# A hybrid attention and FP4 feed-forward kernel: the feed-forward input is turned by DMA, scales are spread by two DMAs, the quantizer works in place with its reciprocals in PSUM

## The chip, the cores and the metric

The kernel runs on one core of a Trainium2 chip. The metric is the device time of one execution in microseconds; less is better. Engines are named as in the profile: PE (TensorE, matmuls; PEld its weight loads), DVE (VectorE), ACT (ScalarE), POOL (GpSimd), SP (SyncE, which issues all DMAs here).

## The reference

x has 4 sequences of 2048 tokens of 256 values, all f32. Four residual steps are applied to it, each on the layer norm of x:

```python
x = x + attn_a(layernorm(x))   # v projection, scaled per head by s / s (s from random feature maps of q and k)
x = x + ffn(layernorm(x))
x = x + attn_b(layernorm(x))   # linear attention across the 4 sequences, per token and head
x = x + ffn(layernorm(x))

def fp4_quant_dequant(x):                     # blocks of 16 along the last dimension
    scale = max(max(abs(xb)) / 6.0, 1e-12)
    q = GRID[searchsorted(MID, abs(xb / scale))] * sign(xb) * scale

def ffn(x):                                   # 256 -> 704 -> 256
    h = silu(fq(x) @ fq(w_gate).T) * (fq(x) @ fq(w_up).T)
    return fq(h) @ fq(w_down).T
```

Here `fq` is `fp4_quant_dequant`. Both the input of the feed-forward part (256 wide) and its hidden values (704 wide) are quantized at run time.

## The kernel before

Tokens go through in 16 groups (`NJ`) of 128 tokens x 4 sequences (`S`). A first pass over x takes the statistics that the first attention needs and quantizes the weights (`quantize`). Then, for each group, come `attention_a`, `ffn_in` and four `ffn_tile`s, `attention_b`, and again `ffn_in` and four `ffn_tile`s: 32 inputs and 128 tiles in all.

Nothing is issued in the order in which the code stands. Each step is an operation of a planner (`Plan.op`): an engine, a cost, a due time (`BEGIN` of its group and stage, plus its place in the stage) and the tiles that it reads and writes. `Plan.order` runs through a model of the engines, takes at each moment the ready operation with the earliest due time, hands out buffers from pools (`plan.pool`, `tiles`), and so writes one fixed order for each engine. `port=True` marks operations that the planner keeps from running on DVE and POOL at the same time. The table `BEGIN` holds six due times for each of the 16 groups.

PSUM has eight banks: four in the pool `mm` (gate and up results, `hidden`), four in `bank` (everything else that PE writes).

The quantizer `to_grid` is a chain: DVE takes the maxima of blocks (L1215) and their reciprocals (L1225), multiplies the values by them (`over_scales`, L390, two SBUF inputs), ACT takes absolute values into bf16 steps (`to_steps`, L396), and DVE rounds by two passes (`to_sum` L403, `from_sum` L406). The values lie in blocks of 17 (`xn`, `h`; the 17th keeps the maxima above zero), the results go to tiles of their own (`qax`, `qa`).

What happens after it differs:

- *The input* (`ffn_in`): the grid values stay f32 in `qax`. ACT multiplies the maxima by 1/6 (L1270), POOL multiplies the values by the scales (`times_scales`, L1278), PE turns them with eight 128x128 transposes into two banks, and ACT copies these into `turned` (`turn`, L1152 and L1159).
- *A tile* (`ffn_tile`): the grid values go to bf16 (`qm`), and one DMA transpose turns them (`gT`, L1513). The maxima are turned by PE (L1294), scaled by ACT on their way to `sT` (L1302), and spread by six DMAs over 16 partitions each into `hqT` (`spread`, L1311). POOL multiplies the two (L1522), and PE takes the product through the down projection (L1559). The last four tiles go another way, with POOL and PE transposes (L1535).

Layer norms are `take_var` (ACT, L348) and `root` (a chain of eight small POOL operations, `take_rstd`).

## Time and profile before

| | |
|---|---|
| three runs | 1486.37, 1483.82, 1482.01 us; median 1483.82 |
| the profiled execution | 1483.54 us, of which 1481.7 us from its first to its last instruction (the span) |
| mean granted TensorE clock | 0.998 of full |
| PE busy | 1436.8 us, 97% |
| DVE, ACT, POOL busy | 1344.0 (91%), 794.4 (54%), 769.7 us (52%) |
| DMA | 33.8% of 16 engines' time; 744 spread DMAs and 124 transposes into tiles |

Busy times are unions of the instructions' intervals on an engine; a group's mean is the time from start to end of one instruction, and pipelined instructions overlap. L numbers are lines of the kernel before. "A <- B" in a list of waits says that A's engine sat idle until B ended.

### The profile page before, as it was taken

Reading aid. Unit: us, or ns where it says so; the run is one execution under the profiler, and the core shown is the slowest. Engines: PE = TensorE matmul, PEld = TensorE weight load, DVE = VectorE, ACT = ScalarE, POOL = GpSimd, SP = SyncE. Lnnn points to the kernel's source line nnn. Section 1 sums busy time; section 2 is a strip of 40 time slices with the busy share of each in tenths; the row PEclk is TensorE's granted clock in tenths of the full one; section 3 lists DMA queues with packets and bytes.
Section 4 is the critical chain, followed back from the end, with each engine's and each line's share of the span. In section 5 each row is a group of like instructions: output and inputs, shape, how many; then the busy total and the mean of one; then the engine's idle time right before and its main releaser. Section 6 shows DMA issues by size and latency. Waiting matters only on the chain.

```text
span 1481.7 us, 19959 instructions
## 1 busy us (share of the span) xinstructions
PE 1436.8 (97%) x5742; PEld 998.8 (67%) x5742; DVE 1344.0 (91%) x2139; ACT 794.4 (54%) x1693; POOL 769.7 (52%) x787
## 2 busy tenths in 40 slices
PE   7989999999999999999999999999999999999998
PEld 6745667666767667676666666676677667676776
DVE  6799999999899999988997999988999898999995
ACT  6656557742674545544376455557525744546332
POOL 5344556534763646454644537556365654564532
PEclk9999999999999999999999999999999999999999
DMA  8402422124324334143432433231344134322451
GB/s 258 120 0 37 65 44 38 35 51 81 61 45 83 65 63 79 36 86 55 89 74 34 65 58 68 46 67 27 60 96 78 38 62 74 63 56 40 92 90 40
DMA packets 220990, 96.87 MB, mean 65 GB/s; under 512 B 108240, under 2 KB 220624, under 8 KB 220880
## 3 DMA queue, kind: packets, MB, share of 16 engines
q1 hardware_dynamic: 220880, 95.60, 33.8%
q8 instruction: 45, 0.74, 0.2%
q14 instruction: 65, 0.53, 0.1%
HBM read 18.09 MB, written 8.39 MB: 18 GB/s over the span
## 4 chain that ended last, share of the span: by engine, by line
PE 67%; DVE 13%; POOL 7%; DMA 5%; issue 4%; ACT 3%; SPq 1%; POOLq 0%; ACTq 0%; DVEq 0%
PE bank L1455 30%; PE bank L1175 17%; PE bank L1559 17%; PE bank L1152 3%; DMA gT<-qm 3%; POOL hqT L1522 2%; DVE qa L403 1%; DVE qm L406 1%; DVE pp L1666 1%; DVE h L1487 1%; DVE sh L1215 1%; DVE qa L390 1%; DVE x L342 1%; POOL norms_f L358 1%; PE bank L1294 1%
## 5 line engine op out<-in xcount | busy, mean ns | idle before, releaser
L1455 PE MATMUL bank<-wguT,turned 128*128 128x352 f32 x2048 | 634.2, 459 | 2.0 <-ACT sil L1476 2.0
L1455 PEld LDWEIGHTS bank<-wguT,turned 128*128 128x128 f32 x2048 | 380.4, 190 | 201.5 <-issue 11.8
L1522 POOL TENSOR_TENSOR hqT<-hqT,gT 128x768 f32<-128x768 f32 x124 | 228.8, 1849 | 258.6 <-DMA gT<-qm 117.4
L1559 PE MATMUL bank<-wdT,hqT 128*128 128x256 f32 x1536 | 350.9, 380 | 7.1 <-POOL hqT L1522 6.6
L1559 PEld LDWEIGHTS bank<-wdT,hqT 128*128 128x128 f32 x1536 | 288.7, 190 | 66.8 <-POOL hqT L1522 16.7
L1476 ACT ACTIVATE sil<-bank 128x352 f32<-128x352 f32 x256 | 115.7, 457 | 131.5 <-PE bank L1455 123.3
L396 ACT ACTIVATE qm<-qa 128x704 bf16<-128x704 f32 (+2 forms) x136 | 106.0, 780 | 96.9 <-DVE qa L390 74.6
L1487 DVE TENSOR_TENSOR h<-sil,bank 128x352 f32<-128x352 f32 x256 | 128.4, 506 | 29.6 <-ACT sil L1476 15.5
L1774 POOL TENSOR_TENSOR pp<-vg,sc 128x1024 f32<-128x1024 f32 x64 | 138.6, 2179 | 22.2 <-DVE tok L1795 20.1
L403 DVE SCALAR_TENSOR_TENSOR qa<-qm,qa 128x704 f32<-128x704 bf16 (+2 forms) x136 | 141.0, 1039 | 7.7 <-ACT qm L396 7.4
L390 DVE SCALAR_TENSOR_TENSOR qa<-sh,h 128x704 f32<-128x704 f32 x128 | 133.4, 1047 | 0.5
L406 DVE SCALAR_TENSOR_TENSOR qm<-qm,qa 128x704 bf16<-128x704 bf16 x124 | 126.8, 1025 | 0.2
L1175 PE MATMUL bank<-wvz,turned 128*128 128x512 f32 x256 | 119.8, 608 | 6.9 <-ACT turned L1159 3.5
L1175 PE MATMUL bank<-wqkB,turned 128*128 128x512 f32 x256 | 120.4, 593 | 1.8 <-ACT turned L1159 1.8
L1159 ACT COPY turned<-bank 128x512 f32<-128x512 f32 x160 | 87.5, 584 | 64.2 <-PE bank L1152 63.8
L1215 DVE TENSOR_REDUCE sh<-h 128x44 f32<-128x748 f32 x128 | 118.3, 924 | 2.0
L1278 POOL TENSOR_TENSOR qax<-qax,sx 128x1024 f32<-128x1024 f32 x32 | 68.1, 2128 | 90.2 <-DVE qax L406 73.8
L348 ACT ACTIVATE dev<-x,norms_f 128x256 f32<-128x256 f32 x128 | 64.7, 506 | 50.5 <-DVE x L342 48.1
L1175 PEld LDWEIGHTS bank<-wvz,turned 128*128 128x128 f32 x256 | 47.6, 193 | 56.9 <-issue 42.5
L1666 DVE TENSOR_TENSOR pp<-qk 128x1024 f32<-128x1024 f32 x64 | 83.2, 1312 | 0.6 <-ACT qk L1654 0.6
L1302 ACT ACTIVATE sT<-bank 44x128 f32<-44x128 f32 x124 | 32.8, 267 | 92.7 <-PE bank L1294 50.8
L384 ACT ACTIVATE xn<-x,norms_f 128x256 f32<-128x256 f32 x128 | 67.5, 593 | 21.3 <-POOL norms_f L378 18.2
(193 smaller groups left out, 2079.3 us busy)
## 6 DMA issues: line engine op xcount, KB each, us to landing
hqT<-sT SPq DMA_DIRECT2D x620, 64.0 KB
x<-in_L_attn_a_x_dram SPq DMA_DIRECT2D x23, 512.0 KB
out_dram<-x SPq DMA_DIRECT2D x64, 128.0 KB
hqT<-sT SPq DMA_DIRECT2D x124, 32.0 KB
gT<-qm SPq DMA_TRANSPOSE x124
hqT<-in_L_ffn_w_down_dram SPq DMA_DIRECT2D x2, 352.0 KB
hqT<-in_L_ffn_w_gate_dram SPq DMA_DIRECT2D x5, 128.0 KB
hqT<-in_L_ffn_w_up_dram SPq DMA_DIRECT2D x5, 128.0 KB
```

What stands on the lines that cost most here:

```text
L390: nc.vector.scalar_tensor_tensor(blocks(a), over_blocks(rs), -6.0 * BELOW, src, ALU.mult, ALU.mult)
L396: nc.scalar.activation(m, a, AF.Abs, scale=UP)
L403: nc.vector.scalar_tensor_tensor(a, m, FLOOR, a, ALU.max, ALU.add)
L406: nc.vector.scalar_tensor_tensor(a if to is None else to, m, FLOOR, a, ALU.max, ALU.subtract)
L1175: nc.tensor.matmul(bank.ap[:, :n], lhs.ap[:, c, s * P : (s + 1) * P], w[:, c, :], start=(c == 0), stop=(c == KC - 1),)
L1215: lambda: nc.vector.tensor_reduce(q.ap[:, 0, :], src.ap, AX.X, ALU.max, apply_absolute_value=True),
L1455: nc.tensor.matmul(bank.ap[:, :HF], xqT.ap[:, c, s * P : (s + 1) * P], w[:, c, cols], start=(c == 0), stop=(c == KC - 1),)
L1476: lambda g=g, sil=sil: nc.scalar.activation(sil.ap, g.ap[:, :HF], AF.Silu),
L1487: lambda u=u, sil=sil, half=half: nc.vector.tensor_mul(h.ap[:, half * FB // 2 : (half + 1) * FB // 2, :BLK], blocks(sil.ap), blocks(u.ap[: ...
L1522: lambda: nc.gpsimd.tensor_mul(hqT.ap, hqT.ap, gT.ap),
L1559: nc.tensor.matmul(o.ap[:, :D], hqT.ap[:, i, :], wdT[:, i, :], start=(i == 0), stop=(i == 5),)
L1774: nc.gpsimd.tensor_mul(pv.ap.rearrange("p t (n e) -> p t n e", e=HD), vg.ap[:, :, :D].rearrange("p t (n e) -> p t n e", e=HD), over_blocks ...
```

## The change

The input of the feed-forward part now goes the way of the tiles: its grid values go to bf16 (`qmx`, in place of the steps), one DMA transpose of eight blocks turns them (`gTx`), the scales are turned by PE and spread by DMA into `turned`, and POOL multiplies there. The spread is made of two DMAs in place of six, for tiles and inputs: ACT first writes each scale twice (by 1/6), PE turns these, ACT copies the turned scales out of PSUM in pieces of 32 rows beside each other, and each DMA spreads 16 of the rows, eight times each, with all pieces in one run. The order of chunks in `hqT` follows from that.

The quantizer works in place, in its 17-wide blocks; `qa` and `qax` are gone, `h` has five buffers and `xn` two. The reciprocals of the maxima go to PSUM: the eighth bank is taken out of the pool `bank` (three are left) and holds two places for inputs (`rx`) and four for tiles (`rh`); `over_scales` is no longer marked `port=True`. The weights' quantizer works in place too, and one of the two banks of the first pass's sums comes from `mm`. `dev`, into which `take_var` writes values that nobody reads, is bf16. Some operations name a buffer as their "place", so that it is handed out earlier. The table `BEGIN` has new values throughout.

```diff
         for j in range(NJ)
     }
-    dev = one([P, D], "dev")
+    dev = one([P, D], "dev", dtype=BF16)
 
...
@@ -388,7 +388,7 @@
     def over_scales(a, src, rs):
 
         nc.vector.scalar_tensor_tensor(
-            blocks(a), over_blocks(rs), -6.0 * BELOW, src, ALU.mult, ALU.mult
+            a, over_blocks(rs), -6.0 * BELOW, src, ALU.mult, ALU.mult
         )
 
     def to_steps(m, a):
@@ -416,24 +416,27 @@
         return made
 
     plan.pool("mm", banks[:4])
-    plan.pool("bank", banks[4:])
+    plan.pool("bank", banks[4:7])
+    plan.pool("rx", [banks[7][:, 64 * i : 64 * i + 64] for i in range(2)])
+    plan.pool("rh", [banks[7][:, 128 + FB * i : 128 + FB * (i + 1)] for i in range(4)])
     plan.pool("x", xs_of)
     tiles("turned", 6, [P, KC, GT], fp)
 
-    floored = tiles("xn", 1, [P, S * D // BLK, BLK + 1], fp)
-    floored += tiles("h", 3, [P, FB, BLK + 1], fp)
-    tiles("qax", 2, [P, S * D], fp)
+    floored = tiles("xn", 2, [P, S * D // BLK, BLK + 1], fp)
+    floored += tiles("h", 5, [P, FB, BLK + 1], fp)
     tiles("qmx", 1, [P, S * D], fp, BF16)
-    tiles("sx", 2, [P, 3, S * D // BLK], fp)
+    tiles("sx", 2, [P, 4 * S * D // BLK], fp)
     tiles("sil", 2, [P, HF], fp)
-    tiles("qa", 3, [P, FF], fp)
 
     for t in tiles("qm", 2, [P, 6 * P], fp, BF16):
         nc.gpsimd.memset(t[:, FF:], 0.0)
     tiles("gT", 2, [P, 6, P], fp, BF16)
 
-    tiles("sT", 2, [FB, P], fp)
-    tiles("sh", 4, [P, 3, FB], fp)
+    tiles("sT", 2, [32, 3, P], fp)
+    tiles("sTx", 1, [32, S, P], fp)
+    tiles("gTx", 1, [P, S * KC, P], fp, BF16)
+    for t in tiles("sh", 4, [P, 2 * FB + 96], fp):
+        nc.gpsimd.memset(t[:, FB : FB + 96], 0.0)
     for t in tiles("hqT", 3, [P, 6, P], fp):
         nc.gpsimd.memset(t[P // 2 :, 5, :], 0.0)
     tiles("tok", 1, [P, S, D], fp)
...
@@ -748,17 +751,17 @@
                 "DVE",
                 0.15 + n / 1000.0,
                 at + 1,
-                lambda: over_scales(ap(a), blocks(ap(raw)), sc(2)),
-                [(raw, 0), (w, 0)],
-                [(a, 0)],
+                lambda: over_scales(blocks(ap(raw)), blocks(ap(raw)), sc(2)),
+                [(w, 0)],
+                [(raw, 0)],
...
@@ -1106,22 +1109,22 @@
 
 
     BEGIN = [
-        (-378, -314, -1376, -1348, 17, -996),
-        (-171, 99, -285, -130, -472, 322),
...
+        (-991, -209, -170, -1464, -194, -968),
+        (-54, 117, -88, -713, 84, 124),
...
@@ -1204,70 +1207,84 @@
                     port=True,
                 )
 
-        def to_grid(at, src, parts, a, m, q, us, to=None):
-
-            v = blocks_of(src)
-            n = us["n"]
+        def to_grid(at, b, parts, m, q, us, to):
+
+
+            n, nb = us["n"], us["n"] // BLK
+            r = plan.buf("rx" if n > FF else "rh")
+
+            def v():
+                return b.ap[:, :, :BLK]
+
+            def mv():
+                return blocks(m.ap[:, :n])
+
             op(
                 "DVE",
                 us["amax"],
                 at,
                 lambda: nc.vector.tensor_reduce(
-                    q.ap[:, 0, :], src.ap, AX.X, ALU.max, apply_absolute_value=True
+                    q.ap[:, :nb], b.ap, AX.X, ALU.max, apply_absolute_value=True
                 ),
-                [(src, i) for i in parts],
+                [(b, i) for i in parts],
                 [(q, 0)],
             )
             op(
                 "DVE",
                 us["recip"],
                 at + 0.5,
-                lambda: nc.vector.reciprocal(q.ap[:, 2, :], q.ap[:, 0, :]),
+                lambda: nc.vector.reciprocal(r.ap, q.ap[:, :nb]),
                 [(q, 0)],
-                [(q, 2)],
+                [(r, 0)],
             )
             op(
                 "DVE",
                 us["pass"],
                 at + 1,
-                lambda: over_scales(a.ap, v(), q.ap[:, 2, :]),
-                [(src, i) for i in parts] + [(q, 2)],
-                [(a, 0)],
-                port=True,
+                lambda: over_scales(v(), v(), r.ap),
+                [(r, 0)],
+                [(b, i) for i in parts],
             )
             op(
                 "ACT",
                 us["abs"],
                 at + 2,
-                lambda: to_steps(m.ap[:, :n], a.ap),
-                [(a, 0)],
+                lambda: to_steps(mv(), v()),
+                [(b, i) for i in parts],
                 [(m, 0)],
             )
             op(
                 "DVE",
                 us["pass"],
                 at + 4,
-                lambda: to_sum(a.ap, m.ap[:, :n]),
+                lambda: to_sum(v(), mv()),
                 [(m, 0)],
-                [(a, 0)],
+                [(b, i) for i in parts],
                 port=True,
             )
             op(
                 "DVE",
                 us["pass"],
                 at + 4.1,
-                lambda: from_sum(a.ap, m.ap[:, :n], to and to.ap[:, :n]),
-                [(a, 0), (m, 0)],
-                [(to or a, 0)],
+                lambda: from_sum(v(), mv(), blocks(to())),
+                [(b, i) for i in parts] + [(m, 0)],
+                [(us["into"], 0)],
                 port=True,
             )
 
...
-        def scales_turned(at, q, dst):
-
-
-            bank, sT = plan.buf("bank"), plan.buf("sT")
+        def scales_turned(at, q, nb, dst, with_it, sT, us, to, spare=None):
+
+
+            bank = plan.buf("bank")
+            n = -(-2 * nb // 32)
+
+            def sd():
+                return q.ap[:, nb : nb + 32 * n]
+
+            op(
+                "ACT",
+                0.15 + nb / 1400.0,
+                at - 0.5,
+                lambda: nc.scalar.mul(
+                    blocks(sd()[:, : 2 * nb], 2),
+                    over_blocks(q.ap[:, :nb], 2),
+                    1.0 / 6.0,
+                ),
+                [(q, 0)],
+                [(q, 1)],
+            )
             op(
                 "PE",
                 0.109,
                 at,
-                lambda: nc.tensor.transpose(bank.ap[:FB, :P], q.ap[:, 0, :], ident),
-                [(q, 0)],
-                [(bank, 0)],
-            )
-            op(
-                "ACT",
-                0.157,
-                at + 0.5,
-                lambda: nc.scalar.mul(sT.ap, bank.ap[:FB, :P], 1.0 / 6.0),
-                [(bank, 0)],
-                [(sT, 0)],
-            )
+                lambda: nc.tensor.transpose(bank.ap[: 32 * n, :P], sd(), ident),
+                [(q, 1)],
+                [(bank, 0), (sT, "place"), (with_it, "place")],
+            )
+            for i in range(n):
+                op(
+                    "ACT",
+                    0.157,
+                    at + 0.5 + 0.1 * i,
+                    lambda i=i: nc.scalar.copy(
+                        sT.ap[:, i, :], bank.ap[32 * i : 32 * i + 32, :P]
+                    ),
+                    [(bank, 0)],
+                    [(sT, i)],
+                )
 
             def spread():
-                for i, f in enumerate(HC):
-                    n = min(P, FF - f) // BLK
-                    src = sT.ap[f // BLK : f // BLK + n]
+                for c in range(2):
                     nc.sync.dma_start(
-                        dst.ap[: n * BLK, i, :], src.unsqueeze(1).to_broadcast([n, BLK, P])
-                    )
-
-            op("SP", 4.9, at + 1, spread, [(sT, 0)], [(dst, "scale")], land=2.7)
-
-        def blocks_of(b):
-            return lambda: b.ap[:, :, :BLK]
-
+                        to(c),
+                        sT.ap[16 * c : 16 * c + 16].unsqueeze(1).to_broadcast([16, 8, n, P]),
+                    )
+
+            op(
+                "SP",
+                1.4,
+                at + 1,
+                spread,
+                [(sT, i) for i in range(n)],
+                [(dst, "scale")],
+                land=us,
+                spare=spare,
+            )
 
         def attention_a(at):
             xT = turn(at, X, range(S), lambda: X.ap, 2)
@@ -1330,7 +1369,7 @@
                     at + 2 + 2 * s,
                     lambda s=s, bank=bank: project(bank, 2 * D, xT, s, wvz),
                     [(xT, 0), (xT, 1), ("wvz z", 0), ("wvz v", 0)],
-                    [(bank, 0)],
+                    [(bank, 0), (vz, "place")],
                 )
 
                 def drain(s=s, bank=bank):
...
@@ -1426,25 +1465,66 @@
                     [(X, s), (key, "rstd")],
                     [(xn, s)],
                 )
+            nb = S * D // BLK
             to_grid(
                 at + 5,
                 xn,
                 range(S),
-                qa,
                 qm,
                 sx,
-                {"amax": 1.19, "recip": 0.475, "pass": 1.13, "abs": 0.95, "n": S * D},
-            )
-            times_scales(at + 11, qa, sx, 1.93)
-            return turn(
-                at + 14, qa, [0], lambda: qa.ap.rearrange("p (s d) -> p s d", s=S)
-            )
+                {
+                    "amax": 1.19,
+                    "recip": 0.475,
+                    "pass": 1.13,
+                    "abs": 0.95,
+                    "n": S * D,
+                    "into": qm,
+                },
+                lambda: qm.ap,
+            )
+            dst, gT = plan.buf("turned"), plan.buf("gTx")
+            scales_turned(
+                at + 7,
+                sx,
+                nb,
+                dst,
+                qm,
+                plan.buf("sTx"),
+                2.7,
+                lambda c: dst.ap[:, c, :].rearrange("p (s n) -> p s n", n=P),
+                {"turned": 1},
+            )
+            op(
+                "SP",
+                1.8,
+                at + 11,
+                lambda: nc.sync.dma_start_transpose(gT.ap, qm.ap),
+                [(qm, 0)],
+                [(gT, 0), (dst, "place")],
+                land=2.3,
+            )
+
+            def scale_input():
+                t = dst.ap.rearrange("p c (s n) -> p s c n", n=P)
+                nc.gpsimd.tensor_mul(t, t, gT.ap.rearrange("p (s c) n -> p s c n", c=KC))
+
+            op(
+                "POOL",
+                1.93,
+                at + 13,
+                scale_input,
+                [(gT, 0), (dst, "scale")],
+                [(dst, 0), (dst, 1)],
+                port=True,
+            )
+            return dst
 
 
         def ffn_tile(at, k, s, xqT):
-            h, qa, qm, sh = (plan.buf(p) for p in ("h", "qa", "qm", "sh"))
+            h, qm, sh = (plan.buf(p) for p in ("h", "qm", "sh"))
 
             apart = (k, j) != (2, NJ - 1)
+            last = None if apart else plan.buf("pp")
             for half in range(2):
                 cols = slice(half * HF, (half + 1) * HF)
                 g, u, sil = plan.buf("mm"), plan.buf("mm"), plan.buf("sil")
@@ -1496,15 +1576,34 @@
                 at + 6,
                 h,
                 range(2),
-                qa,
                 qm,
                 sh,
-                {"amax": 0.85, "recip": 0.35, "pass": 0.8, "abs": 0.68, "n": FF},
-                qm if apart else None,
+                {
+                    "amax": 0.85,
+                    "recip": 0.35,
+                    "pass": 0.8,
+                    "abs": 0.68,
+                    "n": FF,
+                    "into": qm if apart else last,
+                },
+                lambda: (qm.ap if apart else last.ap.rearrange("p s d -> p (s d)"))[:, :FF],
             )
             hqT = plan.buf("hqT")
+
+            def by_chunk(b):
+                return b.ap.rearrange("p (c i) n -> p i c n", c=2)
+
             if apart:
-                scales_turned(at + 8, sh, hqT)
+                scales_turned(
+                    at + 8,
+                    sh,
+                    FB,
+                    hqT,
+                    qm,
+                    plan.buf("sT"),
+                    2.6,
+                    lambda c: hqT.ap[:, 3 * c : 3 * c + 3, :],
+                )
                 gT = plan.buf("gT")
                 op(
                     "SP",
@@ -1512,20 +1611,22 @@
                     at + 14,
                     lambda: nc.sync.dma_start_transpose(gT.ap, qm.ap),
                     [(qm, 0)],
-                    [(gT, 0)],
+                    [(gT, 0), (hqT, "place")],
                     land=1.9,
                 )
                 op(
                     "POOL",
                     1.604,
                     at + 16,
-                    lambda: nc.gpsimd.tensor_mul(hqT.ap, hqT.ap, gT.ap),
+                    lambda: nc.gpsimd.tensor_mul(
+                        by_chunk(hqT), by_chunk(hqT), gT.ap.rearrange("p (i c) n -> p i c n", c=2)
+                    ),
                     [(gT, 0), (hqT, "scale")],
                     [(hqT, 0)],
                     port=True,
                 )
             else:
-                times_scales(at + 12, qa, sh, 1.4)
+                times_scales(at + 12, last, sh, 1.4)
                 for i0, i1 in ((0, 4), (4, 5), (5, 6)):
                     bank = plan.buf("bank")
 
...
@@ -1558,7 +1661,7 @@
                 for i in range(6):
                     nc.tensor.matmul(
                         o.ap[:, :D],
-                        hqT.ap[:, i, :],
+                        hqT.ap[:, 3 * (i % 2) + i // 2, :],
                         wdT[:, i, :],
                         start=(i == 0),
                         stop=(i == 5),
```

## The prediction

> **What bounds the kernel now.** First the page: the busy shares, the throttle's row and the chain that ended last.
>
> ```profile
> PE 1436.8 (97%) x5742; PEld 998.8 (67%) x5742; DVE 1344.0 (91%) x2139; ACT 794.4 (54%) x1693; POOL 769.7 (52%) x787
> ...
> PEclk9999999999999999999999999999999999999999
> ...
> PE 67%; DVE 13%; POOL 7%; DMA 5%; issue 4%; ACT 3%; SPq 1%; POOLq 0%; ACTq 0%; DVEq 0%
> ```
>
> TensorE is busy for 1436.8 of 1481.7 us, and nearly full speed is granted throughout, so its idle time is only 44.9 us. VectorE comes second, at 91%. Where does PE idle? The windows view (length, then busy time of PE, PEld, DVE, ACT, POOL, granted clock, DMA share, GB/s):
>
> ```profile
> 0.00:50.00 50.00, 40.23 (x233) 35.75 (x234) 30.75 (x109) 36.01 (x76) 29.36 (x107) 1.00 0.85 246
> 50.00:100.00 50.00, 46.90 (x195) 29.11 (x194) 47.60 (x106) 20.40 (x48) 14.69 (x18) 1.00 0.12 33
> 100.00:150.00 50.00, 45.03 (x169) 27.87 (x168) 47.21 (x80) 34.75 (x76) 22.25 (x31) 0.97 0.21 30
> ...
> 1450.00:1481.70 31.70, 25.97 (x123) 20.64 (x122) 14.82 (x23) 7.38 (x19) 6.84 (x5) 1.00 0.09 31
> ```
>
> The first 150 us hold 9.8+3.1+5.0 = 17.8 us of PE idle and the last 32 us hold 5.7. The 1300 us between hold only 21.4. There PE always has a next matmul, and work taken off PE shortens the run nearly one for one, if the others keep up.
>
> Next the groups by line, shapes apart (count, busy us, mean ns, then idle time before them and what ended it):
>
> ```profile
> L390 DVE SCALAR_TENSOR_TENSOR qa<-sh,h 128x704 f32<-128x704 f32 x128 | 133.4, 1047 | 0.5
> ...
> L1278 POOL TENSOR_TENSOR qax<-qax,sx 128x1024 f32<-128x1024 f32 x32 | 68.1, 2128 | 90.2 <-DVE qax L406 73.8 <-ACT xn L384 7.4 <-PE bank L1559 3.9
> ...
> L1152 PE MATMUL bank<-ident,qax 128*128 128x128 f32 x256 | 34.6, 275 | 1.7 <-POOL qax L1278 1.7
> ...
> L1302 ACT ACTIVATE sT<-bank 44x128 f32<-44x128 f32 x124 | 32.8, 267 | 92.7 <-PE bank L1294 50.8 <-DMA hqT<-sT 38.5 <-issue 2.5
> ```
>
> They are what the change touches: the first keeps its work and gets another operand, the others go or are replaced. A mean of pipelined transposes is not their pitch; that comes from a row of the timeline (start, length):
>
> ```profile
> 20.22 1.04 PE L1152 MATMUL bank<-ident,x 128*128 128x128 f32 x8
> ```
>
> Eight transposes take 1.04 us, the last of them 0.273 (the median of one) of it, so the pitch is (1.04-0.273)/7 = 0.110 us.
>
> **The change, part by part.**
>
> *PE.* Each of the 32 `ffn_in` loses eight f32 transposes (L1152, `qax`) and gains one, of its scales: 256 x 0.110 = 28.1 us off, 32 x 0.110 = 3.5 us on, net -24.6 us. The transposes of the tiles' scales (L1294) stay 124; each has 96 columns of weights in place of 44, but streams the same 128 columns.
>
> *ACT.* Per tile one copy of 267 ns becomes a multiply (128x88; L1270 at 128x64 took 254, L1716 at 128x128 took 307, so about 280) and three 32-row copies (about 260): +0.80 us x 124 = +99 us. Per input two 584 ns copies and the 254 ns multiply become one of about 307 and four copies: -0.07 us. ACT goes from 794 to about 893 us, 61%. The cover is its idle time: it waited 123 us for PE before L1476 alone. Without that cover the price would be the whole 99.
>
> *Latency of the scales.* A new wait: ACT's multiply waits for VectorE's maxima (L1215), with the next `Silu` (L1476) queued behind it, for which PE's `mm` banks wait; and PE's transpose waits for that multiply, with matmuls behind it. The transpose comes 0.28 us later, and one hand-over (0.04: L1215 ended at 701.67, the load for L1294 began at 701.71). PE and its loads waited 17 times for VectorE before L1294, 12.2 us in all. If those 17 all grow by 0.32 us that is 5.4 us; if the new order puts other work there, 0. I take the middle, +3. Behind the transpose the scales come sooner: six DMA issues of 0.72 us on average on SP (4.7 us) become two (1.4), against two more copies (0.53).
>
> *SP and DMA.* Per tile 4.7+1.45 us of issuing (spread, transpose) become 1.4+1.45; per input two spreads and a transpose of eight blocks are new (1.4, and 8/6 x 1.45 = 1.9). SP issues for 124 x 6.15 = 763 us before, for 124 x 2.85 + 32 x 3.3 = about 460 after. The input's pieces are moved into SP's queue among the tiles' spreads, transposes and output stores, which wait behind them; SP is lighter for all of these. The DMA engines are a third busy (33.8%) and stay near that: 32 x 1024 more transpose packets, fewer and longer spread packets.
>
> *POOL.* The multiply of L1278 (minimum 1927 ns, 128x1024) is replaced by one of equal size on the turned data: 0 in busy time. What changes is its wait: a transpose DMA and the spread, in place of VectorE. Behind it in POOL's queue stand the tile multiplies L1522 and the chains of `root`. Between the issue of a tile's transpose and its multiply lie 2.8 us at least, 4.6 at the median (124 pairs of the trace).
>
> *DVE.* The pass L390 reads its reciprocals from PSUM. The line's own view (minimum/median/maximum ns):
>
> ```profile
> L390 DVE SCALAR_TENSOR_TENSOR qa<-sh,h x128: 819/880/3074, 126.6 to 1460.4; 128x704 f32<-128x704 f32 x128
> ```
>
> and that of L342, the one line with both kinds of operand:
>
> ```profile
> L342 DVE SCALAR_TENSOR_TENSOR x<-bank,x x128: 353/415/425, 143.3 to 1411.8; 128x256 f32<-128x256 f32 x128
> ...
> L342 DVE SCALAR_TENSOR_TENSOR x<-vz,x x64: 359/416/1746, 90.1 to 1164.1; 128x256 f32<-128x256 f32 x64
> ```
>
> With two SBUF inputs single instructions stretch to 1.7 and 3.1 us; with one in PSUM 128 of them never passed 0.425. So the tail of L390 goes: 128 x (1047-880) = 21.4 us, and 0.5 from the 1024-wide ones. The price of PSUM is between -1 ns (the medians of L342) and +49 (734 for the 512-wide L1337 from PSUM, 685 for the 512-wide L390), so up to 16 us for 160 passes and 160 reciprocals, whose writes to PSUM no row shows. I take 0, from the pair that differs in nothing else. DVE then falls from 1344 to 1322 us, about as PE falls (1437 to 1412), and stays as far behind PE as now.
>
> [...]
>
> *PSUM banks.* "bank" falls from four to three. Followed through the trace from first write to last read, the four were in use 1.44 at a time between 150 and 1430 us, and all four for 3.7% of it, 47 us. So the price is between 0 and 47; I take 0, since 64 fills of 1.9 us each, the input's, also go.
>
> *Covered or free.* Work in place, bf16 out of L406 (1025 ns against 1059 for f32 at L403), bf16 `dev`: 0. At the start a raw weight block holds its `hqT` buffer until it is turned: 0 to 8 us (PE's idle from 50 to 150), taken as 0. An input's `turned` buffer is taken some steps sooner; its price is part of the next item.
>
> *The order.* The new table of start times deals the whole order anew. The rows of before can't price that; the 21.4 us of idle in the middle bound what it can win, and I allow as much loss.
>
> Sum against the profiled execution (1483.5 us, the span and 1.8 around it; the median is 0.3 above): 1483.5 - 28.1 + 3.5 + 3 = 1461.9, so 1462.
>
> [...]
>
> **Rivals.**
>
> *A, slower: POOL waits for the input's DMAs and PE waits for POOL.* The place is POOL's in-order queue at the new input multiply. The waits view (total, times, longest):
>
> ```profile
> POOL hqT L1522 <- DMA gT<-qm: 117.4, 32, 10.1
> ...
> POOL hqT L1522 <- DMA hqT<-sT: 65.1, 11, 11.1
> ...
> PEld bank L1559 <- POOL hqT L1522: 16.7, 21, 2.4
> ...
> PE bank L1559 <- POOL hqT L1522: 6.6, 8, 1.6
> ```
>
> A wait for a transpose lasts 117.4/32 = 3.7 us. If all 32 input multiplies wait so, POOL loses 117 us; of its 182.5 us of such waits today 23.3 reached PE and its loads, 13%. At that share the price is 15 us: 1477, still 6.6 faster. It decides from 23% of the 117 on: 26.4 us is what lies between 1461.9 and 1488. At a third, 39 us: 1461.9 + 39 = 1501. Against it: the spread is issued in a third of the time, POOL is idle 48%.
>
> *B, no change: VectorE is the real bound.* For it: 91%, and 46 of 50 us in most windows. If PSUM gives DVE nothing (+16 against -22, or POOL's stalls move to L403 and L406), the PE time freed turns into waits for DVE: about 1482. Against it: of PE's waits only some 10 us end on DVE.
>
> *C, faster still:* the new order also takes up the idle of the middle: 1461.9 - 21.4 = 1440.5 if all of it goes.
>
> **Numbers.** Forecast 0.75, A 0.15, B 0.07, C 0.03. The forecast's own bounds are 1444 (1462 less 18 of the 21.4) and 1483 (1462 and 21.4), and B lies inside, so the range holds 0.82. About 0.3%, 4.5 us, is what can be told from no change. Faster takes the forecast and C: 0.78; same, mostly B: 0.06; slower, A and a little of B: 0.16.
>
> **What would show it.** Right: no transposes of `qax`, PE busy near 1412 us, idle near 48; the 704-wide L390 with no maximum above 1 us; DVE near 1322. Wrong: PE idle above 70 us with L1559 or L1455 released by POOL and a DMA (A); PE busy lower but idle released by DVE (B); waits of PE on bank drains (three banks).

## The result, and the profile after

The changed kernel is slower: 1528.15 us, median of four runs (1526.27 to 1530.87), against 1484.82 us for the kernel before on the same chip; the ratio is 1.0295 with a 95% interval of 1.0269 to 1.0322. The forecast was 1462. Line numbers below are those of the changed kernel, or of the experiment's kernel where one is named: the old L1455, L1522, L1559 and L1278 have become L1535, L1621, L1662 and L1509.

The page of the changed kernel, with the rows that answer to those shown of before, and the row of the DMA queue:

```profile
span 1528.8 us, 18796 instructions
...
PE 1439.6 (94%) x5518; PEld 979.1 (64%) x5518; DVE 1329.0 (87%) x2139; ACT 893.5 (58%) x2133; POOL 724.1 (47%) x794
...
PEclk9999999999999999999999999999999999999999
...
q1 hardware_dynamic: 206848, 124.83, 47.9%
...
PE 37%; DVE 21%; DMA 14%; POOL 10%; ACT 9%; issue 7%; SPq 1%; POOLq 0%; ACTq 0%; DVEq 0%
```

PE does 224 matmuls less and is as long busy as before; its idle time has doubled, from 44.9 to 89.2 us. In the chain that ended last PE falls from 67% to 37%, and DMA and POOL together rise from 12% to 24%. The DMA engines, which were to stay near 33.8%, are at 47.9%.

The windows view of the changed kernel (columns as before):

```profile
50.00:100.00 50.00, 46.81 (x207) 29.93 (x205) 43.96 (x103) 22.49 (x51) 12.64 (x15) 1.00 0.10 27
100.00:150.00 50.00, 43.30 (x144) 26.00 (x145) 47.81 (x76) 34.54 (x83) 21.78 (x25) 0.93 0.48 74
150.00:1430.00 1280.00, 1218.61 (x4571) 821.23 (x4570) 1134.63 (x1741) 761.52 (x1823) 625.92 (x615) 0.99 0.48 79
```

The start is as it was, 10.3 + 3.2 + 6.7 = 20.2 us of PE idle in the first 150 (17.8 before). The middle has 61.4 us in 1280, where before had 21.4 in 1300. So the loss is spread over the steady part, and VectorE has slack there too. The waits view (total, times, longest) says on whom:

```profile
POOL hqT L1621 <- DMA gT<-qm: 201.5, 47, 10.9
POOL hqT L1621 <- DMA hqT<-sT: 129.6, 23, 17.4
...
PEld bank L1662 <- POOL hqT L1621: 58.4, 45, 3.6
...
POOL turned L1509 <- DMA gTx<-qmx: 42.4, 10, 9.3
...
PE bank L1662 <- POOL hqT L1621: 36.0, 36, 3.1
POOL turned L1509 <- DMA turned<-sTx: 35.6, 9, 14.5
```

POOL waits 331.1 us for a tile's two DMAs (182.5 before) and 78.0 for the input's two, which are new. PE and its loads wait 94.4 us for the tile's product (23.3 before) and 16.2 for the input's; loads overlap PE's own work (PEld is busy 64% of the span, PE 94%), and PE by itself waits 42.2 us for the two products (8.2 before), most of the 44.3 us that its idle time grew by. This is the place and the kind of rival A. The section of DMA issues (KB each, median us from issue to landing) shows what is long:

```profile
hqT<-sT SPq DMA_DIRECT2D x248, 192.0 KB, 4.2
turned<-sTx SPq DMA_DIRECT2D x64, 256.0 KB, 5.3
...
gT<-qm SPq DMA_TRANSPOSE x124, 3.2
```

The order of instructions was written with two spreads landing 1.4 + 2.6 = 4.0 us after the first issue (the constants in the diff; 1.4 + 2.7 = 4.1 for an input). In the trace it is 5.3 us for a tile's pair and 6.4 for an input's, at the median. One such case, from the chain of the changed kernel (start, length, what):

```profile
405.30 0.59 SPq L1344
...
405.94 6.93 DMA turned<-sTx
...
413.03 2.44 POOL turned L1509
415.47 0.81 POOL norms_b L367
```

POOL stands for the input's scales until 413 us, and the layer norm behind them in its queue is held too.

### The profile page after: what moved, and what is told of

Its sections match the earlier page's. It is cut to its first block, busy times and chain, and to the rows that moved or that the text cites. A ratio compares the mean times of both kernels' runs of the same rounds, so it can differ in the third digit from the quotient of the medians.

```text
span 1528.8 us, 18796 instructions
## 1 busy us (share of the span) xinstructions
PE 1439.6 (94%) x5518; PEld 979.1 (64%) x5518; DVE 1329.0 (87%) x2139; ACT 893.5 (58%) x2133; POOL 724.1 (47%) x794
## 2 busy tenths in 40 slices
DMA packets 206951, 126.03 MB, mean 82 GB/s; under 512 B 141568, under 2 KB 198400, under 8 KB 206848
## 3 DMA queue, kind: packets, MB, share of 16 engines
q1 hardware_dynamic: 206848, 124.83, 47.9%
## 4 chain that ended last, share of the span: by engine, by line
PE 37%; DVE 21%; DMA 14%; POOL 10%; ACT 9%; issue 7%; SPq 1%; POOLq 0%; ACTq 0%; DVEq 0%
PE bank L1535 14%; PE bank L1662 10%; PE bank L1178 10%; DMA gT<-qm 7%; POOL hqT L1621 4%; DMA hqT<-sT 2%; DVE sh L1226 2%; DVE h L1567 2%; DMA turned<-sTx 2%; DVE x L342 2%; DVE h L390 2%; DVE qm L406 2%; DVE h L403 1%; PE bank L582 1%; POOL turned L1509 1%
## 5 line engine op out<-in xcount | busy, mean ns | idle before, releaser
L1535 PE MATMUL bank<-wguT,turned 128*128 128x352 f32 x2048 | 639.5, 462 | 9.6 <-POOL turned L1509 6.2
L1535 PEld LDWEIGHTS bank<-wguT,turned 128*128 128x128 f32 x2048 | 381.1, 191 | 213.9 <-issue 12.6
L1662 PE MATMUL bank<-wdT,hqT 128*128 128x256 f32 x1536 | 361.6, 387 | 37.7 <-POOL hqT L1621 36.0
L1621 POOL TENSOR_TENSOR hqT<-hqT,gT 128x768 f32<-128x768 f32 x124 | 216.8, 1751 | 364.6 <-DMA gT<-qm 201.5
L1662 PEld LDWEIGHTS bank<-wdT,hqT 128*128 128x128 f32 x1536 | 291.4, 193 | 109.9 <-POOL hqT L1621 58.4
L396 ACT ACTIVATE qm<-h 128x704 bf16<-128x704 f32 x128 | 100.7, 788 | 104.7 <-DVE h L390 52.5
L1556 ACT ACTIVATE sil<-bank 128x352 f32<-128x352 f32 x256 | 115.0, 459 | 67.1 <-PE bank L1535 61.4
L403 DVE SCALAR_TENSOR_TENSOR h<-qm,h 128x704 f32<-128x704 bf16 x128 | 132.9, 1043 | 21.3 <-ACT qm L396 21.1
L1335 ACT COPY sT<-bank 32x128 f32<-32x128 f32 x372 | 94.7, 255 | 49.3 <-PE bank L1326 41.3
L406 DVE SCALAR_TENSOR_TENSOR qm<-qm,h 128x704 bf16<-128x704 bf16 x124 | 122.4, 992 | 0.5
L1509 POOL TENSOR_TENSOR turned<-turned,gTx 128x1024 f32<-128x1024 f32 x32 | 72.2, 2257 | 102.9 <-DMA gTx<-qmx 42.4
L390 DVE SCALAR_TENSOR_TENSOR h<-bank,h 128x704 f32<-128x704 f32 x128 | 112.9, 882 | 1.4
L1769 DVE TENSOR_TENSOR pp<-qk 128x1024 f32<-128x1024 f32 x64 | 81.3, 1291 | 10.4 <-ACT qk L1757 10.3
L1314 ACT ACTIVATE sh<-sh 128x88 f32<-128x88 f32 x124 | 33.9, 273 | 96.1 <-DVE sh L1226 95.8
L348 ACT ACTIVATE dev<-x,norms_f 128x256 bf16<-128x256 f32 x128 | 64.8, 506 | 33.4 <-DVE x L342 30.2
```

Source lines behind the costliest of these rows:

```text
L390: nc.vector.scalar_tensor_tensor(a, over_blocks(rs), -6.0 * BELOW, src, ALU.mult, ALU.mult)
L396: nc.scalar.activation(m, a, AF.Abs, scale=UP)
L403: nc.vector.scalar_tensor_tensor(a, m, FLOOR, a, ALU.max, ALU.add)
L406: nc.vector.scalar_tensor_tensor(a if to is None else to, m, FLOOR, a, ALU.max, ALU.subtract)
L1535: nc.tensor.matmul(bank.ap[:, :HF], xqT.ap[:, c, s * P : (s + 1) * P], w[:, c, cols], start=(c == 0), stop=(c == KC - 1),)
L1556: lambda g=g, sil=sil: nc.scalar.activation(sil.ap, g.ap[:, :HF], AF.Silu),
```

## The experiments

Theory: the new spread is the loss. Two DMAs that each read 16 neighbouring partitions land later than the order allows for, the transposes behind them in the queue come late too, and POOL hands this on to PE. Rivals: the reciprocals in PSUM (operand price, or the lost bank), the new order whatever the DMAs do, and the input's detour alone. All kernels but the last keep the changed kernel's order of instructions to the letter, so that only the durations differ.

**Rows at every other partition.** The scales are written in another order, so that each DMA reads 16 of the 32 rows at every other partition. Bytes, packets and destinations are the same.

```diff
             def sd():
-                return q.ap[:, nb : nb + 32 * n]
+                return q.ap[:, 16 * n : 48 * n]
...
                 lambda: nc.scalar.mul(
-                    blocks(sd()[:, : 2 * nb], 2),
-                    over_blocks(q.ap[:, :nb], 2),
+                    sd().rearrange("p (i b t c) -> p i c b t", b=8, t=2, c=2),
+                    q.ap[:, : 16 * n]
+                    .rearrange("p (i c b) -> p i c b", c=2, b=8)
+                    .unsqueeze(4)
+                    .to_broadcast([P, n, 2, 8, 2]),
...
-                        sT.ap[16 * c : 16 * c + 16].unsqueeze(1).to_broadcast([16, 8, n, P]),
+                        sT.ap[c::2].unsqueeze(1).to_broadcast([16, 8, n, P]),
```

> The changed kernel with its order of instructions kept; the rows that one spread DMA reads lie at every other partition of 32, not at 16 neighbours. Theory 1 (late landing: the order was made for spreads that land 2.6 us after issue, and they land after 4.2): if neighbours are what makes a 1536-byte packet take 158 ns, packets get shorter, landing comes near 3.3 us and the time falls to 1500 to 1515. Rival 2 (three banks, or the extra ACT work, stall PE): packets may change, the time stays at 1524 to 1532. If packets stay at 158 ns, neighbours are not the reason, and the time says nothing.

Measured: 1474.62 us (1472.25 to 1477.15), ratio to before 0.9934 (0.991 to 0.9958). This one edit of where the rows lie turns 2.95% slower into 0.7% faster, 53.5 us in all. The order of instructions and the three banks are the changed kernel's, so neither of them alone is the cause of these 53.5 us. Its page, waits and DMA issues:

```profile
PE 1421.6 (97%) x5518; PEld 975.8 (66%) x5518; DVE 1317.0 (90%) x2139; ACT 893.5 (61%) x2133; POOL 727.0 (49%) x794
...
q1 hardware_dynamic: 206848, 124.83, 41.8%
```

```profile
POOL hqT L1624 <- DMA gT<-qm: 160.4, 41, 9.7
...
POOL hqT L1624 <- DMA hqT<-sT: 95.1, 18, 16.9
...
PEld bank L1665 <- POOL hqT L1624: 26.5, 28, 2.7
...
PE bank L1665 <- POOL hqT L1624: 10.7, 18, 2.1
```

```profile
hqT<-sT SPq DMA_DIRECT2D x248, 192.0 KB, 3.1
turned<-sTx SPq DMA_DIRECT2D x64, 256.0 KB, 3.8
...
gT<-qm SPq DMA_TRANSPOSE x124, 2.9
```

A tile's pair now lands after 3.9 us, just within the 4.0 of the order, an input's after 4.7 (4.1); PE and its loads wait 37.2 us for the tile's product in place of 94.4, and PE's idle time is 48.6 us, near the 44.9 of before. The queue moved the same 206848 packets in 41.8% of the engines' time in place of 47.9%: a packet of 1536 bytes took 130 ns in place of 158, one of 2048 bytes 171 in place of 225.

**Which of the two spreads.** The same edit for the tiles alone (`n == 3`), then for the inputs alone (`n == 4`), in ACT's multiply and here:

```diff
-                        sT.ap[16 * c : 16 * c + 16].unsqueeze(1).to_broadcast([16, 8, n, P]),
+                        (sT.ap[c::2] if n == 3 else sT.ap[16 * c : 16 * c + 16])
+                        .unsqueeze(1).to_broadcast([16, 8, n, P]),
```

> The changed kernel, order kept; only the tiles' spreads (124 pairs) read rows at every other partition, the inputs' (32 pairs) read 16 neighbours as in the change. Theory 1a (the tiles' lateness, 1.3 us each, is most of the 53 us that both together gave): 1478 to 1492. Theory 1b (the inputs' lateness, 2.3 us each, which holds up four tiles, is most of it): 1500 to 1525.

> The changed kernel, order kept; only the inputs' spreads read rows at every other partition. Theory 1a: 1512 to 1525. Theory 1b: 1478 to 1500. If the gains of this run and of the one with the tiles alone add up to more than 53 us, the two latenesses hide each other; if to less, they feed each other.

Measured: 1501.28 us (1500.11 to 1503.69) with the tiles' rows apart, 1515.62 (1513.67 to 1516.05) with the inputs'. They bring 26.9 and 12.5 us, together 39.4 of the 53.5: both are part of the cause, the tiles more. Each lateness costs less while the other is there too: the tiles' is worth 41.0 us with the inputs in time (1515.62 - 1474.62) and 26.9 with them late, the inputs' 26.7 and 12.5. So the two hide each other in part; the expectation had read a sum below 53 us as the opposite.

**A spread of a third of the bytes.** Each DMA carries one of its three or four pieces; the rest of the scales is left out, and VectorE sets the tiles' buffers to zero at the start.

```diff
-                        to(c),
-                        sT.ap[16 * c : 16 * c + 16].unsqueeze(1).to_broadcast([16, 8, n, P]),
+                        to(c)[:, :1, :],
+                        sT.ap[16 * c : 16 * c + 16, :1].unsqueeze(1).to_broadcast([16, 8, 1, P]),
```

> The changed kernel, order kept; each spread DMA moves only its first piece (a third of a tile's scales, a quarter of an input's), and the rest of the scales is left out. Theory 1: spreads land about 2 us after issue, as early as the order wants them; PE's waits for POOL go and the time falls to 1465 to 1490. Rival 2: PE goes on waiting for banks or ACT, above 1515. Rival 3 (the transposes, not the spreads, are late): 1495 to 1520, POOL still waits for transposes.

Measured: 1483.72 us, ratio 0.9987 (0.9971 to 1.0002). Landing falls to 2.4 us, and POOL's waits for the tile's DMAs to 230.6 us. The issuing is the same, so the loss is in the transfer. It is not faster than with the rows apart, although the scales come sooner: VectorE's `pp<-qk` multiply went from a mean of 1237 ns there to 1342 here. In the traces 22 of the 64 multiplies run beside POOL work in each kernel, at a mean of 1284 ns there and 1591 here; the other 42 take 1212 in both. That this makes the 9 us between the two kernels is not shown. Landing earlier than the order needs bought nothing.

**Six DMAs for a tile, the number before the change.** Each reads eight rows, at every other partition of 16 (before: eight neighbours). The rest is left as changed.

```diff
+                    if n == 3:
+                        for i in range(n):
+                            nc.sync.dma_start(
+                                to(c)[:, i, :],
+                                sT.ap[16 * c : 16 * c + 16 : 2, i].unsqueeze(1).to_broadcast([8, 16, P]),
+                            )
+                        continue
```

> The changed kernel, order kept; a tile's scales are spread by six DMAs from 8 rows each, as before the change, an input's by two. Theory 1: the last piece lands about 7 us after the first issue in place of 5.3, transposes queue behind: 1550 to 1600. Rival 2: no change, 1524 to 1532. If two large DMAs are themselves the harm, faster than 1520.

Measured: 1585.9 us (1580.88 to 1589.01), 58 above the changed kernel. POOL waits 197.0 us for the spreads (129.6), PE 66.7 us for the product (36.0). In an order written for two, six issues make POOL and PE wait longer still; merging them was a help here.

**The reciprocals back in SBUF.** The eighth bank stays empty, so that the pools are the same; first with the changed kernel's spread, then with the rows at every other partition.

```diff
-    plan.pool("rx", [banks[7][:, 64 * i : 64 * i + 64] for i in range(2)])
+    plan.pool("rx", [t[:, 192:256] for t in tiles("sx", 2, [P, 4 * S * D // BLK], fp)])
...
-    plan.pool("rh", [banks[7][:, 128 + FB * i : 128 + FB * (i + 1)] for i in range(4)])
+    plan.pool("rh", [t[:, FB + 96 :] for t in sh_tiles])
```

> The changed kernel, order kept; the reciprocals lie in SBUF again (in unused columns of the tiles of maxima), and the eighth bank stands empty. Theory 1: DVE gets the stalls of its first pass back (some 20 us) but is not what PE waits for most: 1528 to 1545. Rival 2b (reading and writing PSUM slows DVE): faster than 1520.

> The kernel with all rows apart (1474.6 us), order kept, with the reciprocals in SBUF again and the eighth bank empty. If the prediction's term holds (21 us of DVE's stalls, DVE close behind PE): 1490 to 1500. If a stall also moves what waits for DVE, as in the run with the reciprocals in SBUF and late DMAs (42 us): 1505 to 1520. If DVE is not on the path when the DMAs land in time: 1474 to 1480.

Measured: 1570.37 us (1566.47 to 1573.06) against 1528.15, and with the rows apart 1535.63 (1534.64 to 1537.86) against 1474.62. The edit that a rival blamed is worth 42 and 61 us in this order. The view of line L390 (minimum/median/maximum ns), of the changed kernel and then of the one with the reciprocals in SBUF:

```profile
L390 DVE SCALAR_TENSOR_TENSOR h<-bank,h x128: 820/882/893, 129.8 to 1511.9; 128x704 f32<-128x704 f32 x128
```

```profile
L390 DVE SCALAR_TENSOR_TENSOR h<-sh,h x128: 821/893/2766, 130.7 to 1549.9; 128x704 f32<-128x704 f32 x128
```

From PSUM no instruction of 128 passes 0.893 us; from SBUF the median is 11 ns higher, but the longest takes 2.8 us and the mean is 1295 ns (1047 before the change, where the planner keeps POOL away from it by `port=True`). In the trace of the kernel before, 65 of the 128 ran beside POOL work even so, at a mean of 1214 ns, and the other 63 took 875; in the changed kernel, with an operand in PSUM, 86 ran beside POOL work at a mean of 883 ns, and the other 42 took 878.

**How the rows are dealt.** Each DMA reads only eight rows, sixteen times each (the scales that arrive are those of other blocks): first eight neighbours, then every fourth of the 32.

```diff
-                        sT.ap[16 * c : 16 * c + 16].unsqueeze(1).to_broadcast([16, 8, n, P]),
+                        sT.ap[16 * c : 16 * c + 8].unsqueeze(1).to_broadcast([8, 16, n, P]),   # neighbours
+                        sT.ap[c::4].unsqueeze(1).to_broadcast([8, 16, n, P]),                  # apart
```

> Each spread DMA reads eight neighbouring rows of the turned scales sixteen times each, in place of sixteen rows eight times: same bytes, same packets, same destination, same order (the scales that arrive are those of other blocks). The runs so far: 192 KB landed 4.2 us after issue from 16 neighbouring rows, 3.1 from 16 rows at every other partition, and 64 KB from 16 neighbouring rows 2.4. If what counts is over how many groups of eight neighbouring partitions the rows are dealt (two and four so far), these three give 1.5 us and 192 KB at 71 KB/us from two groups and at about 120 from four, so 30 to 35 from each; then one group needs 1.5 + 192 / 33 = about 7 us, and the kernel is far slower than the changed one: 1.1 us of landing cost 53 us, so 2.8 more cost some 100 to 140, 1630 to 1670 us. Rival: it is neighbouring rows as such, however many; then landing stays near 4.2 us and the time near 1528.

> Each spread DMA reads eight rows, sixteen times each, at every fourth of the 32 partitions, so two in each of four groups of eight (again the scales that arrive are those of other blocks). If the number of groups counts, landing is as with sixteen rows at every other partition: about 3.1 us for a tile and 3.8 for an input, and the time about 1475 us. Rival: the number of reads of each row counts (sixteen in place of eight), and then landing is longer than 3.1 us, and if that alone made the 1.1 us, above 4.2, and the time above 1528.

Measured, one run each: 1962.83 us for the neighbours, 1495.26 for every fourth. Landing is not recorded for these; from the first packet of a tile's pair to the end of its last it was 7.4 us for eight neighbours, 3.4 for sixteen (the changed kernel), 2.2 for sixteen at every other partition, and 2.4 for eight at every fourth. With the number of rows held, the spacing alone turns 7.4 us into 2.4, and 3.4 into 2.2. The size was underestimated, 1963 against 1630 to 1670, with the granted clock down to 0.903. The rows at every fourth came 20 us above those at every other partition; an input's pair took 3.7 us from first to last packet there, against 2.9. The faster of the two has the larger share of the DMA engines' time, 41.8% against 34.9%.

The rival, neighbours as such, does not fall by this. During a tile's spread 5.4 packets are under way at once at the median in the trace of the kernel before, whose DMAs read eight rows each, and 11.5 in that of the changed kernel, with sixteen; for the eight neighbours 256 packets of 179 ns at the mean in 7.4 us make 6.2, an estimate. So eight neighbours would be about half as fast as sixteen even if a packet took the same time (it took 179 ns, against 158). The eight rows at every fourth are as many for each DMA, and are three times as fast as the eight neighbours (2.4 us against 7.4): the number of rows is not alone what holds those back.

As 384 KB (of 1024 bytes) over these times, a tile's pair moved 52 KB/us from eight neighbours for each DMA, 113 from sixteen, and 171 and 159 with the rows apart: the rate grows with the spread of the rows. Counted by groups of eight neighbouring partitions (one, two, four for each DMA) that is some 55 a group up to two, and 40 to 43 with four; why it is less there was not tried. This count is an estimate: it takes the pair's DMAs as running in turn, and in the changed kernel the first lands 3.75 us after its issue and the second 1.3 us after that, so they overlap in part.

Nor do the runs tell groups of eight neighbours from smaller ones: counted by fours, the rows of a DMA lie in two, four and eight groups, and 52 and 113 KB/us are 26 and 28 for each of the first two, an estimate of the same kind. Which groups they are was not tried.

**An order written for the landings.** With the rows apart, the constants of the input's steps are set to what they took, and `BEGIN` is searched anew for them in the planner's model.

```diff
-                2.7,
-                lambda c: dst.ap[:, c, :].rearrange("p (s n) -> p s n", n=P),
+                3.3,
+                lambda c: dst.ap[:, c, :].rearrange("p (s n) -> p s n", n=P),
...
-                1.93,
+                2.06,
                 at + 13,
```

> The kernel with the rows at every other partition (1474.6 us), with an order written for what the input's steps took there: the spread's landing 3.3 us in place of 2.7 after its issues, POOL's input multiply 2.06 us in place of 1.93, and a new table BEGIN found for these by a search in the planner's model. Theory: what is left between 1474.6 and the forecast 1462 is idle time from an order written for shorter landings of the input; then PE's idle falls from 48.6 us towards 40 and the time to 1460 to 1470. Rival: what is left lies in things that the order's due times don't reach (single transposes of the scales, the start, POOL's waits for VectorE), or the model's errors elsewhere eat the gain: 1470 to 1485, so nothing that can be told from 1474.6, or a little slower.

Measured: 1485.77 us, ratio 1.0002 (0.9987 to 1.0018). PE's idle is 57.7 us, and the rival's outcome came, at its slower end: a better order in the model is not one on the chip at this size. The version with the rows apart and the change's own table stays the fastest, 0.7% ahead of the kernel before.

| kernel | us | against before |
|---|---|---|
| changed | 1528.15 | 1.0295 |
| rows at every other partition | 1474.62 | 0.9934 |
| tiles' rows apart alone | 1501.28 | 1.0104 |
| inputs' rows apart alone | 1515.62 | 1.0199 |
| a third of the spread's bytes | 1483.72 | 0.9987 |
| six DMAs for a tile | 1585.9 | 1.068 |
| reciprocals in SBUF | 1570.37 | 1.058 |
| rows apart, reciprocals in SBUF | 1535.63 | 1.0335 |
| rows apart, new order | 1485.77 | 1.0002 |

## Why the prediction was wrong

*SP and DMA* is the step that failed: the sum holds no term for the landing of the spreads, and dealing the rows apart gave 53.5 us back. It counted the issuing (4.7 us become 1.4) and took the transfer as given: "the DMA engines are a third busy and stay near that: fewer and longer spread packets". Longer packets were no cheaper by the byte: 512 bytes took 44 ns before, 1536 bytes 158 ns, where three times 44 is 133. The tiles' and inputs' spread packets sum to 31744 x 158 + 8192 x 225 ns over 16 engines = 429 us, where before 87296 x 44.2 gave 241; 16.8 MB of that is the inputs' spread, for which the text had issue times and no transfer. With the rows apart the 1536 bytes took 130 ns, so the price by the byte was that of before. The text looked at a queue and at shares of time, and not at which partitions the packets come from. The share itself is not the harm: with the rows apart it was 41.8%, also far above 33.8%, and the kernel was fast.

From there *latency of the scales* fell with it: "behind the transpose the scales come sooner". From the first issue to the last packet a tile's spread took 7.1 us before, 4.9 after: sooner indeed, but the order had been written anew for 4.0 to landing, and it landed after 5.3. The order before allowed 4.9 + 2.7 = 7.6 us (the old constants in the diff), and there the last packet came within them at the median. What counts is not whether a transfer is faster than it was, but whether it meets the time that a written-out order gives it.

*Rival A* had the mechanism, with the wrong share; its sign came, PE idle above 70 us and released by POOL and a DMA. Its premise was 117 us of new waits at the input alone, of which 13% reach PE, "decides from 23%". The input's waits came to 78.0 us, the tiles' rose by 148.6. PE and its loads waited 110.6 us for POOL's two products, against 30.1 before (23.3 for the tile's, 6.8 for `qax`): 80.5 of 226.6 us came through, 36% by the prediction's own count (of PE's own idle, 34.0 us). With the rows apart POOL waits 324.4 us for these DMAs, 142 more than before, and PE and its loads 42.4 us for POOL, 12.3 more: 9%. So the share is no constant of the kernel. A reading that fits, and was not tried further, is that POOL's slack takes the first lateness and PE gets the rest. A share read at one load should not have been carried to another.

Point by point, the other terms:

- *PE, -24.6.* Right in kind: the eight transposes of 32 inputs are gone, 28.7 us from start to start, and the new single ones took 5.6 (3.5 forecast, at the pitch of transposes that follow each other). But PE's busy time is 1439.6 and not 1412 us. It is 1421.6 with the rows apart. The 18 us between the two come with the waits: the mean granted clock is 0.991 in one and 0.998 in the other, by which 1439.6 x 0.007 = 10 us is an estimate for the clock. The down projection's matmuls are longer too, 387 ns at the mean (L1662) against 381 (L1665), of which the clock would make 3 by the same estimate; what makes the rest is not shown.
- *The transposes of the scales, +3.* It did not come: PE and its loads waited 12.2 us before the tiles' (for VectorE) in the kernel before and 5.7 (for ACT) after, with 2.9 for the inputs' new ones.
- *ACT, +99 off the path.* Right: 893.5 us, and its waits for PE absorbed it: those before `Silu` fell from 123.3 to 61.4 us.
- *DVE.* Right: the tail of L390 is gone, 133.4 to 112.9 us, DVE at 1329 (1322 forecast). PSUM cost the pass 2 ns at the median (882 against 880) and the reciprocals 9 (430 against 421 for a tile's), so the price taken as 0 is about 1.7 us for 160 of each. In this order the edit was worth more than forecast, 42 to 61 us.
- *POOL, 0 in busy time.* Nearly: the input's multiply takes 2257 ns at the mean in place of 2128, 4 us in all.
- *PSUM banks, 0.* PE's waits for ACT's copies out of its banks (`turned`, `sT`, `sTx`) were 6.4 us before, 13.1 after and 9.0 with the rows apart. So if all of it is banks the price is 3 to 7 us, not 0; the fourth bank by itself was not tried.
- *The order.* It keeps its promise only if the landings are met. With them met the change gives 1474.6, 12.6 above the forecast: PE idle 48.6 as forecast (48), PE busy 9 us above 1412, the single transposes 1.5 to 2 of it and the rest in steps of under 2 us over several groups of matmuls. That rest stays open.

*Rival B* does not fit: DVE is at 87%, below the 91% of before. The range ended at 1483, the forecast and the 21.4 us of idle in the middle; A's price at 13%, 1477, lay inside it, and what A would cost at a larger share was left to a chance of 0.15. The measured 1528 is beyond even the 1501 that it gave for a third.

## What to carry to other kernels

Where the rows lie that a DMA copies from SBUF to SBUF cost time here: a packet of 1536 bytes took 158 ns from 16 neighbouring partitions and 130 from every other one of 32, and the kernel 1528.15 and 1474.62 us. So deal the rows over the partitions before counting the descriptors. Where an order is written out ahead, compare each transfer's measured landing with what the order supposes, term by term; from the rows apart to the changed kernel POOL waited 84.7 us more for these DMAs, and PE and its loads 68.2 us more for POOL, so a lateness that is small in a table can come through for the most part. And one operand of VectorE's in PSUM was worth far more here than its own speed shows: it cost the pass 2 ns at the median and was worth 42 and 61 us of the kernel, where in the kernel before the pass with its operands in SBUF took 1214 ns beside POOL work and 875 without.

## What the runs showed that was not expected

- The same 206848 packets took 47.9% or 41.8% of the DMA engines' time, and the kernel 1528 or 1475 us, by the source's partitions alone; from eight neighbours the kernel took 1963.
- The mean granted TensorE clock was lower where PE waited more: 0.998 at 48.6 us of idle, 0.991 at 89.2, 0.978 with six DMAs (124.9), 0.903 with eight neighbours (391). The runs of the kernel before alone lie between 0.994 and 1.000, so small steps of this say little. Which of the two draws the other was not tried.
- A shorter spread (landing after 2.4 us) was 9 us slower than one after 3.1, with VectorE's `pp<-qk` longer by 105 ns at the mean, all of it in those that ran beside POOL work (1591 against 1284 ns).
